# The second attention's output projection: six of eight head groups as one sum of two-level seven-product block multiplications

## The chip, the cores and the metric

The kernel runs on one core of a Trainium2 chip. The metric is the device time of one execution in microseconds (us); lower is better. All data are float32, and a matmul of float32 appears in the profile as two records. The engines are TensorE (PE; its weight loads are PEld), VectorE (DVE), ScalarE (ACT), GpSimd (POOL) and SyncE (SP), which issues nearly all DMAs.

## The reference, cut to what matters

Two decoder layers run over x of 4 x 256 tokens with 512 features, each an attention and a feed-forward part with a residual and a layernorm behind. The change is in the second layer's attention: 32 heads of value width 128, and an output projection `wo` of 4096 x 512.

```python
def _L1_attn_ref(hidden_states, wq, wkv, wo):
    ...
    probs = jax.nn.softmax(scores, axis=-1)
    attn = jnp.einsum('bhqk,bkhd->bqhd', probs, v).reshape(B, S, H * DV)
    return jnp.einsum('bse,ed->bsd', attn, wo)
...
x = _layernorm(x + _L1_attn_ref(x, L1_attn_wq, L1_attn_wkv, L1_attn_wo), axis=-1)
x = _layernorm(x + _L1_ffn_ref(x, ...), axis=-1)
```

The projection is one matrix product of 1024 tokens x 4096 by 4096 x 512. The kernel cuts the 4096 into eight groups `r` of four heads (512 rows each).

## The kernel before

The second layer's attention (from L1070) works in eight groups of four heads. While the softmax of group g runs, TensorE also makes the queries and keys of group g + 1; the units of that side work are spread over the sixteen (head, batch) steps `i` of the loop at L1546. Each step's result `att` goes by DMA to `attd[g]` in HBM (`output1`, L1442). In the last group the side work is the end of the queries and keys, and the projection of groups 0 and 1.

The projection of a group is `stages_o` (L1335): a block product after Winograd's form of Strassen's scheme. The left side is the group's attention output, transposed, 512 rows x 1024 tokens; the right side is `wo1[r]`, 512 x 512. Each is cut in two both ways, and seven products of blocks (256 rows x 512 tokens by 256 x 256) give what eight would. `ahead` (L1339) makes the sums and differences that the products need: four of 128x512 on the weights and four of 128x1024 on the attention output, on GpSimd (for group 0, the latter on VectorE). `product` (L1365) issues four matmuls of 256 columns for two token tiles; a group has two stages (`t0` of 0 and 2) of seven products, 56 matmuls. PSUM has three banks for it, and each product is evacuated at once: `plus` (L1377) adds it to the residual `x` on VectorE (L1379), and `last` adds the first product, kept in SBUF as `p1`, to three blocks of `x` on GpSimd (L1389).

Groups 2 to 7 follow behind the attention, one after the other (loop at L1631), with TensorE's program full of products; the next group's loads (`o_load`, `Weights.load`) and combinations run under them. Behind the last group come the layernorm of `x`, its transposes (`turned`), and the second feed-forward part: `routing` and `expert_linear` for each of the eight token tiles.

Where `pinned[0]` is set, instructions stay in program order on their engine; elsewhere the framework may reorder them by its own estimate. Tiles of a pool with the same tag share `bufs` buffers, and a new tile waits until the old one's readers are done; `slot` tiles come from a list of free numbers.

Of the kernel before, what the change touches and what calls it, by code (L numbers as in the profile page):

```python
# [9 lines left out]
F32 = mybir.dt.float32  # L10
# [3 lines left out]
ALU = mybir.AluOpType  # L14
# [3 lines left out]
P = 128  # L18
# [21 lines left out]
def tile_decoder2(ctx: ExitStack, tc: tile.TileContext, a: dict, out: bass.AP):  # L40
# [125 lines left out]
    def thirds(c):  # L166
        return [c[:, i] for i in range(3)]
# [904 lines left out]
    with tc.tile_pool(name="l1", bufs=2) as l1, tc.tile_pool(name="l1x", bufs=1) as l1x:  # L1072
# [250 lines left out]
        def o_load(r):  # L1323

            if r == 0:
                ov[0] = l1.tile([P, GH, N], F32, tag="v", name="att0")
                xo = l1x.tile([P, 5 * GH, Q], F32, tag="x2o", name="xo")
                ov[1] = xo[:, :4 * GH].rearrange("p (h t) c -> p h (t c)", t=4)
                odd = [xo[:, 4 * GH:], *(wts.tile([P, 4, Q], F32, tag=f"x2{i}", name=f"xo{i}", bufs=1) for i in (2, 0))]
                ov["c"] = ([  # L1330
                    l1x.tile([P, 2, HN], F32, tag=f"t{i}", name=f"to{i}") for i in (1, 3, 5)
                ], [t.rearrange("p (h t) c -> p h (t c)", t=2) for t in odd])
            nc.sync.dma_start(out=ov[r % 2], in_=attd[r])

        def stages_o(pr, r):  # L1335

# [118 lines left out]
        for g in range(NG):  # L1455
# [14 lines left out]
            if g > 1:  # L1470
# [2 lines left out]
                    nc.sync.dma_start(out=v[g], in_=vd[g])  # L1473

                sk[0]["load"] = values_of
        so = [stages_o(Weights(a["wo1"][r]), r) for r in range(NG)]
        flat = [st for grp in groups + [rest] + so for st in grp]
        for st, nxt in zip(flat, flat[1:]):
            if "ahead" in nxt and nxt is not so[0][0]:
                st["next"] = nxt["ahead"]  # L1480
        flat[0]["next"] = flat[3]["ahead"]
        del flat[2]["next"]
        for r in range(1, NG - 1):
            so[r][0]["att"] = lambda r=r: o_load(r + 1)
            so[r][0]["load"] = so[r + 1][0]["w"]

        def back(t0):

            for t in (t0, t0 + 2):
# [44 lines left out]
        for u, _ in units_of(groups[0]):  # L1534
            u()


        pending = turned_ = None
        for g in range(NG):
# [6 lines left out]
            for i in range(GH * B):  # L1546
# [11 lines left out]
                if last and i == 1:  # L1558
# [4 lines left out]
                    so[0][0]["ahead"]()  # L1563
                    o_load(1)
                    back(0)
        output1(*turned_)
        output1(*pending[:2], transposes1(pending[2]))


        iscale = 1.0 / math.sqrt(DK)  # L1570
        free[:] = [n for n in range(NSLOT) if n not in (*even, 5, 6, 7, 8)]

        def wslot(shape, src):
            t = slot(len(free), shape)
            nc.sync.dma_start(out=t, in_=src)
            return t

        wqk = [wslot([P, 2, 2 * E * DK], a["wqk"][:, 2 * k:2 * k + 2, :]) for k in range(2)]
        wA, wB = wslot([P, DC, E * R], a["wA"]), wslot([P, D], a["wB"])
        fb = wslot([P, D], a["rows"][:, 2, :])  # L1580
        wf = l1.tile([P, DC, D], F32, tag="v", name="wf")
        nc.sync.dma_start(out=wf, in_=a["wf"])

        def routing(t):

            xts = [xT[:, d, bass.ts(t, P)] for d in range(DC)]
            pqk = bank(f"b{t % 2}", (P, 2, E * DK))
            mm(pqk, [(xts[d], wqk[d // 2][:, d % 2, :]) for d in range(DC)])
            qs = l1.tile([P, E * DK], F32, tag="s5", name="qs", bufs=1)
            A.copy(qs, pqk[:, 0, :])  # L1590
            qk = l1.tile([P, E, DK], F32, tag="s6", name="qk", bufs=1)
            V.tensor_tensor(qk.rearrange("p e d -> p (e d)"), pqk[:, 1, :], qs, ALU.mult)
            se = small.tile([P, E], F32, name="se")
            V.tensor_reduce(se, qk, AX.X, ALU.add)
            nmx = small.tile([P, 1], F32, name="nmx1")
            V.tensor_reduce(nmx, se, AX.X, ALU.max, negate=True)
            nms = small.tile([P, 1], F32, name="nms")
            V.tensor_scalar(nms, nmx, iscale, None, ALU.mult)
            we = small.tile([P, E], F32, name="we")
            sm = small.tile([P, 1], F32, name="sm1")  # L1600
            A.activation(we, se, AF.Exp, bias=nms, scale=iscale, accum_out=sm)
            rc = small.tile([P, 1], F32, name="rc1")
            V.reciprocal(rc, sm)
            wn = small.tile([P, E], F32, name="wn")
            V.tensor_scalar(wn, we, rc, None, ALU.mult)
            return wn

        def expert_linear(t, wn, parts):
            xts = [xT[:, d, bass.ts(t, P)] for d in range(DC)]
            ph = bank("b2", (P, E, R))  # L1610
            mm(ph, [(xts[d], wA[:, d, :]) for d in range(DC)])
# [6 lines left out]
            G.tensor_tensor(x[:, t, :], x[:, t, :], fb, ALU.add)  # L1618

            st = small.tile([P, parts, 6], F32, name="sth")  # L1620
            for k in range(parts):
                cols = bass.ts(k, D // parts)
                po = bank("b2" if k else "o", (P, D // parts))
                mm(po, [(xts[d], wf[:, d, cols]) for d in range(DC)] + [(hwT, wB[:, cols])])
# [5 lines left out]
        halves = ((0, 1, 4, 5), (2, 3, 6, 7))  # L1630
        for r in range(2, NG):  # L1631
            for n, st in enumerate(so[r]):
                for u, _ in units_of([st]):
                    u()
                if r == NG - 1:
                    for t in halves[n]:
                        layernorm(t)
        for t in halves[0]:
            turned(t, A.copy)
        order = (*halves[0], *halves[1])  # L1640
        wn = routing(order[0])
        for n, t in enumerate(order):
            now = wn
            if n in (1, 2):
                for t1 in halves[1][2 * n - 2:2 * n]:
                    turned(t1, A.copy)
            if n + 1 < NT:
                wn = routing(order[n + 1])
            expert_linear(t, now, 2 if n == NT - 1 else 1)


def _layouts(i):
# [86 lines left out]
```

## Time and profile before

| | |
|---|---|
| time, median of 3 runs | 1588.53 us (1587.66 to 1590.2) |
| the profiled execution's own time | 1589.84 us |
| its span from the first to the last instruction | 1587.7 us |
| granted TensorE clock in it | 0.997 |
| busy: PE, DVE, ACT, POOL | 97%, 67%, 46%, 68% |
| projection of groups 2 to 7 | 1361.4 to 1506.45 us of the span |
| from there to the end | 81.25 us |

How to read the views that are shown below. The page's first part has the busy time of each engine. The chain that ended last follows the work back from the last instruction; in order of time, a line has the start, the length, the engine, the tile and the line of the kernel. A timeline line has start, length, engine, line, operation, out<-in and shape. A group line has the count, then busy time in us and the mean in ns of one, then the idle time before and what ended it. Matmuls are pipelined, so their recorded durations overlap and the distance between starts tells the rate.

### The profile page before, as it was taken

The numbers are of one execution on the slowest core, as the hardware profiler recorded it, in microseconds if no ns is written. First come the engines' busy times: TensorE is split into PE (matmuls) and PEld (weight loads), VectorE is DVE, ScalarE is ACT, GpSimd is POOL, SyncE is SP. The second block draws the span as 40 slices with busy tenths as digits, with TensorE's granted clock in tenths as the row PEclk, the third lists the DMA queues.
The fourth block names the chain that finished last, engine by engine and source line by source line (L and its number), as shares of the span: only waits on it lengthen the run. The fifth ranks groups of instructions, "written<-read, shape, count | busy, mean of one in ns | idle before, by whom it ended". The sixth has DMA issues, their size and how long they took to land.

```text
span 1587.7 us, 23217 instructions
## 1 busy us (share of the span) xinstructions
PE 1546.6 (97%) x7549; PEld 1221.9 (77%) x7549; DVE 1066.4 (67%) x2282; ACT 723.3 (46%) x2097; POOL 1084.3 (68%) x1299
## 2 busy tenths in 40 slices
PE   8999999999989999999999999999999999999998
PEld 5566666666567778888789999999999988888854
DVE  2677777776786577777777777777777775333454
ACT  1466666666664341111155555555555543100143
POOL 1988887883077148878687776868677777698520
PEclk9999999999999999999999999999999999999999
DMA  9365655552123036777332523425243154534000
GB/s 346 140 210 202 228 207 213 211 209 93 47 87 122 21 103 201 233 251 228 113 92 71 183 105 120 145 81 170 78 165 126 60 212 140 180 120 151 1 21 33
DMA packets 96620, 227.07 MB, mean 143 GB/s; under 512 B 10096, under 2 KB 53104, under 8 KB 90480
## 3 DMA queue, kind: packets, MB, share of 16 engines
q1 hardware_dynamic: 94832, 224.74, 41.4%
q8 instruction: 62, 1.02, 0.3%
q10 hardware_dynamic: 1664, 0.81, 0.2%
q14 instruction: 62, 0.51, 0.1%
HBM read 140.58 MB, written 84.93 MB: 142 GB/s over the span
## 4 chain that ended last, share of the span: by engine, by line
PE 61%; DVE 3%; POOL 2%; issue 1%; ACT 0%; DVEq 0%; ACTq 0%; POOLq 0%
PE ps_b L1183 21%; PE ps_b L1370 12%; PE ps_s L82 5%; PE ps_b L1280 5%; PE ps_o L1446 3%; PE ps_t L1437 3%; PE ps_t L1280 2%; PE ps_o L82 2%; PE ps_o L53 2%; PE ps_b L82 2%; PE ps_o L1447 2%; PE ps_o L1280 1%; PE ps_s L1280 1%; DVE x L1112 0%; DVE vb L1112 0%
## 5 line engine op out<-in xcount | busy, mean ns | idle before, releaser
L1419 ACT ACTIVATE pr<-ps_s,nmx 128x128 f32<-128x128 f32 (+1 forms) x256 | 105.3, 418 | 140.7 <-DVE nmx L1415 140.6
L1379 DVE TENSOR_TENSOR x<-ps_b,x 128x512 f32<-128x512 f32 x96 | 66.3, 691 | 109.3 <-PE ps_b L1370 101.9
L378 ACT ACTIVATE pr<-ps_s,ebias 128x256 f32<-128x256 f32 x256 | 118.0, 473 | 45.6 <-DVE ebias L373 43.7
L82 PE MATMUL ps_s<-kT,qh 128*128 128x256 f32 x512 | 128.6, 392 | 0.8 <-ACT pr L378 0.8
L82 PEld LDWEIGHTS ps_s<-kT,qh 128*128 128x128 f32 x512 | 91.7, 189 | 36.7 <-issue 20.2
L1112 DVE SCALAR_TENSOR_TENSOR x<-ps_b,p 128x512 f32<-128x512 f32 (+1 forms) x159 | 96.5, 608 | 21.7 <-PE ps_b L1183 9.5
L1431 ACT ACTIVATE pr<-pr,rc 128x128 f32<-128x128 f32 (+1 forms) x256 | 103.7, 455 | 14.2 <-DVE rc L1429 13.3
L160 POOL TENSOR_TENSOR ws<-ws 128x128 f32<-128x128 f32 (+1 forms) x128 | 70.8, 571 | 46.6 <-DMA ws<-in_wq 27.2
L393 DVE TENSOR_SCALAR pr<-pr,rc 128x256 f32<-128x256 f32 x192 | 98.9, 541 | 4.4
L367 DVE TENSOR_REDUCE nmx<-ps_s 128x2 f32<-128x512 f32 x128 | 85.0, 684 | 23.3 <-PE ps_s L82 22.8
L1439 DVE COPY pT<-ps_t 128x384 f32<-128x384 f32 x128 | 71.3, 557 | 35.5 <-PE ps_t L1437 33.6
L1389 POOL TENSOR_TENSOR x<-x,po 128x512 f32<-128x512 f32 x48 | 60.4, 1271 | 35.4 <-DVE x L1379 29.4
L1415 DVE TENSOR_REDUCE nmx<-ps_s 128x1 f32<-128x128 f32 (+1 forms) x256 | 79.5, 352 | 3.4
L1411 DVE TENSOR_TENSOR ps_s<-ps_s,mask 128x256 f32<-128x256 f32 x128 | 55.2, 431 | 36.5 <-PE ps_s L82 36.3
L1446 PE MATMUL ps_o<-pT,v 128*128 128x256 f32 x256 | 76.3, 380 | 0.1
L1112 DVE SCALAR_TENSOR_TENSOR x<-ps_b,x 128x512 f32<-128x512 f32 (+1 forms) x106 | 64.1, 607 | 17.0 <-PE ps_b L1183 10.6
L1109 ACT ACTIVATE p<-ps_b 128x512 f32<-128x512 f32 (+1 forms) x78 | 43.1, 553 | 69.7 <-PE ps_b L1183 36.3
L419 PEld LDWEIGHTS ps_o<-pT,cN 128*64 128x64 f32 x504 | 31.0, 136 | 55.4 <-issue 26.2
L419 PE MATMUL ps_o<-pT,cN 128*64 128x256 f32 x504 | 68.3, 391 | 4.3 <-DVE pT L406 4.3
L163 POOL TENSOR_TENSOR ws<-ws,ws 128x128 f32<-128x128 f32 (+1 forms) x128 | 70.4, 564 | 2.5
L162 POOL TENSOR_TENSOR ws<-ws 128x128 f32<-128x128 f32 (+1 forms) x128 | 71.0, 570 | 1.3
L161 POOL TENSOR_TENSOR ws<-ws 128x128 f32<-128x128 f32 (+1 forms) x128 | 69.8, 563 | 1.3
(699 smaller groups left out, 4495.2 us busy)
## 6 DMA issues: line engine op xcount, KB each, us to landing
attd<-att SPq DMA_DIRECT2D x128, 128.0 KB, 1.8
vw<-ws SPq DMA_DIRECT2D x56, 256.0 KB, 2.4
qd<-ws SPq DMA_DIRECT2D x56, 256.0 KB, 2.2
qb<-vw SPq DMA_DIRECT2D x28, 512.0 KB, 4.6
qb<-qd SPq DMA_DIRECT2D x24, 512.0 KB, 4.4
v<-vd SPq DMA_DIRECT2D x6, 2048.0 KB, 8.8
qc<-vw SPq DMA_DIRECT2D x28, 384.0 KB, 4.2
vw<-ws SPq DMA_DIRECT2D x24, 384.0 KB, 2.5
```

The source lines that it names most:

```text
L82: T.matmul(o, l, r, start=(i == 0), stop=(i == len(pairs) - 1))
L367: V.tensor_reduce(nmx[:, i, :], sc, AX.X, ALU.max, negate=True)
L378: A.activation(pr[:, i, qt, :], sc[:, qt, :], AF.Exp, bias=bias[:, i, qt:qt + 1], accum_out=sm[:, i, qt:qt + 1],)
L393: V.tensor_scalar(prs, prs, rc[:, i, qt:qt + 1], None, ALU.mult)
L419: T.matmul(po[i * RKV:(i + 1) * RKV, :], cN[:, 2 * b + kt, :], pTs[i][:, kt, :], start=(kt == 0), stop=(kt == 1),)
L1112: V.scalar_tensor_tensor(o[key], acc, scale, o[other], ALU.mult, ALU.add)
L1183: T.matmul(acc[:, e, :], pr.inner[i][k], inner[i][k], start=first and e == 0, stop=True, skip_group_check=True,)
L1280: T.matmul(acc[:, t, :].rearrange("p (h c) -> p h c", h=2), inner[i][k][:, t * P:(t + 1) * P], pr.inner[i][k], start=first and t == 0, sto ...
L1370: T.matmul(st[tag][:, tt, :], box["left"][i][:, k, (t0 + tt) * P:(t0 + tt + 1) * P], box["right"][i][:, k, :], start=first and tt == 0 and ...
L1419: A.activation(pr[:, pt, :], sc[:, pt, :], AF.Exp, bias=nmx[:, qt:qt + 1], accum_out=sm[:, qt:qt + 1],)
L1431: A.activation(pr[:, pt, :], pr[:, pt, :], AF.Copy, scale=rc[:, qt:qt + 1])
L1446: T.matmul(po, v[g][:, 2 * b, hv], pT[:, 0:2, :], start=True, stop=False)
```

## The change

Groups 0 and 1 stay as they were. Groups 2 to 7 are done together, and each by two levels of the seven-product scheme: the outer blocks are 256 rows x 512 tokens and 256 x 256, as before, and each of the seven outer products is done by seven inner ones (128 rows x 256 tokens by 128 x 128), 49 in all. The outer products are taken in four passes `p`, `OUTER = ((2, 0), (1, 4), (3, 6), (5,))`, and each pass goes through the six groups: 24 steps `(p, r)`. In a pass each inner product (of a pair of outer ones) has a PSUM bank to itself, in which it is summed over the six groups; `evacuate(p)` empties them behind the pass's last group. `sweep` issues a step's matmuls of 128 columns, 28 for a pair, 14 in the last pass.

The combinations are made in place where they can be: `base_left` and `outer_left` on GpSimd, on the loaded blocks of attention output; `base_right` and `outer_right` on VectorE, on the weights. `prepare_step` makes a step's inner combinations on VectorE, into the double-buffered tiles `c` and `cc`, one step ahead. `jobs` places the rest behind the steps. The sums of evacuated products are kept in `xs` and added to `x` by `post`. Part of the loads is moved into the last attention loop (`o_early`), the rest is queued behind step 0, and the last part's weights behind step 19. The last two attention outputs are done within step 0, and the layernorm and the transposes of tiles 0 to 3 within steps 19 to 23. `pinned[0]` is set throughout.

```diff
-            nc.sync.dma_start(out=ov[r % 2], in_=attd[r])
+            nc.sync.dma_start(out=ov[r], in_=attd[r])
...
-        so = [stages_o(Weights(a["wo1"][r]), r) for r in range(NG)]
+        so = [stages_o(Weights(a["wo1"][r]), r) for r in range(2)]
...
-        for r in range(1, NG - 1):
-            so[r][0]["att"] = lambda r=r: o_load(r + 1)
-            so[r][0]["load"] = so[r + 1][0]["w"]
...
+        RS = range(2, NG)
+        W = D // 4
+        LEFT = {0: (0, 0), 1: (0, 0), 2: (0, 1), 3: (1, 0), 4: (1, 0), 5: (1, 1), 6: (0, 1)}
+        RIGHT = {0: (0, 0), 2: (1, 0), 3: (0, 0), 4: (0, 1), 5: (1, 0), 6: (1, 1)}
+        JS = (0, 1, 4, 2, 6, 3, 5)
+        steps = [(p, r) for p in range(len(OUTER)) for r in RS]
+        L, RW, whole, u2s, combos, acc, spare = {}, {}, {}, {}, {}, {}, {}
+
+        def load_left(r, m, k, t):
+            b = t.rearrange("p (h c) -> p h c", h=2)
+            nc.sync.dma_start(out=b, in_=attd[r][:, 2 * k:2 * k + 2, m * HN:(m + 1) * HN])
+            L[r, m, k] = b
+
+        def load_right(r, n, t):
+            b = t.rearrange("p (h c) -> p h c", h=GH)
+            nc.sync.dma_start(out=b, in_=a["wo1"][r][:, :, 2 * n * W:2 * (n + 1) * W])
+            RW[r, 0, n], RW[r, 1, n], whole[r, n] = b[:, :2], b[:, 2:], b
+
+        def spot():
+            return l1.tile([P, N], F32, tag=f"s{free.pop(0)}", name="ob", bufs=1)
+
+        def base_left(r, m):
+
+            for k in range(2):
+                b = L[r, m, k]
+                G.tensor_tensor(b[:, 0, Q:], b[:, 0, Q:], b[:, 1, Q:], ALU.add)
+
+        def base_right(r, n):
+            b = whole[r, n].rearrange("p (k h) c -> p k h c", k=2)[:, :, 0, :]
+            V.tensor_tensor(b[:, :, W:], b[:, :, W:], b[:, :, :W], ALU.subtract)
+
+        def outer_left(r, which):
+            l11, l12, l21, l22 = (L[r, m, k] for m in range(2) for k in range(2))
+            o, l, rr, op = dict(
+                sum=(l21, l21, l22, ALU.add), s2=(l11, l21, l11, ALU.subtract),
+                s4=(l12, l12, l11, ALU.subtract), s3=(l21, l22, l11, ALU.subtract),
+            )[which]
+            G.tensor_tensor(o, l, rr, op)
+
+        def outer_right(r):
+            base_right(r, 1)
+            r11, r12, r21, r22 = (RW[r, k, n] for k in range(2) for n in range(2))
+            u2 = u2s[r] = wts.tile([P, 2, 2 * W], F32, tag="qc", name="u2", bufs=3)
+            V.tensor_tensor(r12, r12, r11, ALU.subtract)
+            V.tensor_tensor(u2, r22, r12, ALU.subtract)
+            V.tensor_tensor(r11, u2, r11, ALU.subtract)
+            V.tensor_tensor(r21, r21, u2, ALU.subtract)
+
+        def prepare_step(s):
+
+            p, r = steps[s]
+            if p == 0:
+                base_right(r, 0)
+            c = cmb.tile([P, 2, 3, Q], F32, tag="c", name="oc")
+            cc = cmb.tile([P, 2, 3, W], F32, tag="cc", name="occ")
+            for e, i in enumerate(OUTER[p]):
+                b = u2s[r] if i == 1 else RW[(r, *RIGHT[i])]
+                r11, r12, r21, r22 = b[:, 0, :W], b[:, 0, W:], b[:, 1, :W], b[:, 1, W:]
+                u2, u3, u4 = thirds(cc[:, e])
+                V.tensor_tensor(u2, r22, r12, ALU.subtract)
+                V.tensor_tensor(u3, u2, r11, ALU.subtract)
+                V.tensor_tensor(u4, r21, u2, ALU.subtract)
+                b = L[(r, *LEFT[i])]
+                l11, l12, l21, l22 = b[:, 0, :Q], b[:, 1, :Q], b[:, 0, Q:], b[:, 1, Q:]
+                s2, s3, s4 = thirds(c[:, e])
+                V.tensor_tensor(s2, l21, l11, ALU.subtract)
+                V.tensor_tensor(s4, l12, s2, ALU.subtract)
+                V.tensor_tensor(s3, l22, s2, ALU.subtract)
+                combos[s, e] = ((l11, s2, l12, s3, l21, l22, s4), (r11, u2, r21, u3, r12, u4, r22))
+
+        def sweep(s, js=JS):
+
+            p, r = steps[s]
+            pair = OUTER[p]
+            for j in js:
+                fresh = False
+                if r == RS[0]:
+                    k = JS.index(j)
+                    fresh = len(pair) == 2 or k % 2 == 0
+                    if fresh:
+                        spare[p] = bank("q", (P, 2, 2, W))
+                    acc[p, j] = spare[p] if len(pair) == 2 else spare[p][:, k % 2:k % 2 + 1]
+                for e in range(len(pair)):
+                    l, rr = combos[s, e]
+                    for t in range(2):
+                        T.matmul(
+                            acc[p, j][:, e, t, :], l[j][:, t * P:(t + 1) * P], rr[j],
+                            start=fresh and e == t == 0, stop=r == RS[-1], skip_group_check=True,
+                        )
+
+        def evacuate(p):
+
+            n = len(OUTER[p])
+            pick = (slice(0, 2), slice(0, 3, 2), slice(0, 3, 2), slice(0, 1))[p]
+            c00, c01, c10, c11 = (
+                spare["x"][:, pick, 2 * m:2 * m + 2, k * W:(k + 1) * W] for m in range(2) for k in range(2)
+            )
+            held = l1.tile([P, 2, 2, W], F32, tag="p1", name="held")[:, :n]
+            A.copy(held, acc[p, 0])
+            for o, j, other in (
+                (c10, 1, held), (c11, 4, c10), (c00, 2, held), (c01, 6, c11), (c11, 3, c11), (c10, 3, c10), (c10, 5, c10),
+            ):
+                V.tensor_tensor(o, acc[p, j], other, ALU.add)
+
+        def xb(m, k):
+            return x[:, 4 * m:4 * m + 4, 2 * k * W:2 * (k + 1) * W]
+
+        def post(eng, o, k):
+            eng.tensor_tensor(o, o, spare["x"][:, k], ALU.add)
+
+        def early(r, t):
+            load_left(r, 0, 0, t[0])
+            load_left(r, 0, 1, t[1])
+            load_right(r, 0, t[2])
...
+        o_early = {
+            3: lambda: (early(2, (xT[:, 0, :], xT[:, 1, :], qb())), early(3, (xT[:, 2, :], xT[:, 3, :], qb()))),
+            7: lambda: early(4, (spot(), spot(), qb())),
+            9: lambda: early(5, (spot(), spot(), tb(1))),
+            11: lambda: (early(6, (spot(), spot(), tb(3))), base_left(2, 0), base_left(3, 0)),
+            13: lambda: prepare_step(0),
+            15: lambda: prepare_step(1),
+        }
+
+        def o_rest():
+
+            vx, vy = (l1.tile([P, DC, N], F32, tag="v", name="ov") for _ in range(2))
+            for n, r in enumerate((2, 3)):
+                free.insert(0, even[n])
+                load_left(r, 1, 0, spot())
+                load_left(r, 1, 1, vy[:, n, :])
+            pinned[0] = True
+            ring.update(q=[0, 1, 2, 3, 4, 6, 5, 7], t=[5])
+            sweep(0, JS[:5])
+            output1(*turned_)
+            pT = transposes1(pending[2])
+            sweep(0, JS[5:6])
+            output1(*pending[:2], pT)
+            sweep(0, JS[6:])
...
+            for n, r in enumerate(RS):
+                for k in range(2 if r in last_left else 0):
+                    load_left(r, 1, k, last_left[r][k])
+                load_right(r, 1, last_right[n])
+                if r == 3:
+                    early(7, seven_)
+
+            jobs = {s: [] for s in range(len(steps))}
+            for n, r in enumerate(RS):
+                if r > 3:
+                    jobs[n - 2].append(lambda r=r: base_left(r, 0))
+            for n, r in enumerate(RS):
+                jobs[n + 1].append(lambda r=r: (base_left(r, 1), outer_left(r, "sum")))
+                jobs[(4, 5, 6, 7, 7, 8)[n]].append(lambda r=r: outer_left(r, "s2"))
+                jobs[(2, 3, 4, 7, 8, 9)[n]].append(lambda r=r: outer_right(r))
+                jobs[9 + n].append(lambda r=r: outer_left(r, "s4"))
+                jobs[10 + n].append(lambda r=r: outer_left(r, "s3"))
+            jobs[8].append(lambda: post(G, xb(0, 0), 0))
+            jobs[9].insert(0, lambda: post(G, xb(0, 0), 1))
+            jobs[13] += [
+                lambda: V.tensor_tensor(xs[:, 1], xs[:, 1], xs[:, 0], ALU.add),
+                lambda: V.tensor_tensor(xs[:, 2], xs[:, 2], xs[:, 1], ALU.add),
+            ]
+            jobs[15].append(lambda: post(G, xb(0, 1), 2))
+            jobs[16].append(lambda: post(G, xb(1, 1), 2))
+            jobs[18] += [
+                lambda: (post(V, xb(0, 1), 2), post(G, xb(1, 1), 0)),
+                lambda: G.tensor_tensor(xs[:, 1], xs[:, 1], xs[:, 0], ALU.add),
+                lambda: post(G, xb(1, 0), 1),
+            ]
+            jobs[19] += [last_weights, lambda: (layernorm(0, True), layernorm(2))]
+            jobs[20] += [lambda: (layernorm(1, True), layernorm(3))]
+            jobs[21] += [lambda: turned(0, A.copy), lambda: turned(2, A.copy)]
+            jobs[22] += [lambda: turned(1, A.copy)]
+            jobs[23] += [lambda: turned(3, A.copy)]
+            for s in range(len(steps)):
+                p, r = steps[s]
+                if s == 18:
+                    ring["t"] = [1, 2]
+                if s:
+                    sweep(s)
+                if s + 1 < len(steps) and s:
+                    prepare_step(s + 1)
+                if r == RS[-1]:
+                    evacuate(p)
+                for job in jobs[s]:
+                    job()
+            post(V, xb(1, 0), 0)
+            pinned[0] = False
...
+                if last and i in o_early:
+                    o_early[i]()
+        o_rest()
-        output1(*turned_)
-        output1(*pending[:2], transposes1(pending[2]))
...
-        for r in range(2, NG):
-            for n, st in enumerate(so[r]):
...
+        for t in range(4, NT):
+            layernorm(t)
+        ring.update(b0=[3], b1=[4], b2=[6], o=[5], t=[1, 2])
+        wn = routing(0)
...
```

More of the change, by code (lines that the diff above doesn't have):

```diff
@@ L1535, in tile_decoder2, with last_weights, load @@
             u()
+        last_w = {}
+        def last_weights():
+            def load(n, shape, src):
+                t = l1.tile(list(shape), F32, tag=f"s{n}", name="lw", bufs=1)
+                nc.sync.dma_start(out=t, in_=src)
+                return t
+            last_w["wqk"] = [load(k, [P, 2, 2 * E * DK], a["wqk"][:, 2 * k:2 * k + 2, :]) for k in range(2)]
+            last_w["wA"], last_w["wB"] = load(2, [P, DC, E * R], a["wA"]), load(3, [P, D], a["wB"])
+            last_w["fb"] = load(4, [P, D], a["rows"][:, 2, :])
+            last_w["wf"] = [load(9 + k, [P, 2, D], a["wf"][:, 2 * k:2 * k + 2, :]) for k in range(2)]
@@ new lines, in xb, with qb, tb @@
+        def xb(m, k):
[6 more added lines that the diff above has]
+            load_right(r, 0, t[2])
+        def qb():
+            return wts.tile([P, N], F32, tag="qb", name="ow", bufs=3)
+        def tb(k):
+            return l1x.tile([P, N], F32, tag=f"t{k}", name="ow")
@@ new lines, in tile_decoder2 @@
+        o_early = {
[20 more added lines that the diff above has]
+            sweep(0, JS[6:])
+            w = l1.tile([P, 2, N], F32, tag="w", name="ow", bufs=1)
+            xo = l1x.tile([P, 5 * GH, Q], F32, tag="x2o", name="ox")
+            xs = xo.rearrange("p (k t) c -> p k t c", t=GH)
+            spare["x"] = xs[:, :3]
+            last_right = [w[:, 0, :], w[:, 1, :]] + [xs[:, k].rearrange("p t c -> p (t c)") for k in (3, 4)]
+            last_right += [wts.tile([P, N], F32, tag=f"x2{i}", name="ow", bufs=1) for i in (2, 0)]
+            seven_ = (spot(), spot(), tb(5))
+            last_left = {4: (spot(), vy[:, 2, :]), 5: (spot(), vy[:, 3, :]), 6: (vx[:, 0, :], vx[:, 1, :]), 7: (vx[:, 2, :], vx[:, 3, :])}
+            for n, r in enumerate(RS):
[46 more added lines that the diff above has]
+            pinned[0] = False
@@ L1565, in tile_decoder2 @@
                     back(0)
-        output1(*turned_)
-        output1(*pending[:2], transposes1(pending[2]))
+                if last and i in o_early:
+                    o_early[i]()
+        o_rest()
         iscale = 1.0 / math.sqrt(DK)
[L1571 to L1582, printed above, removed]
         def routing(t):
@@ L1587, in routing @@
             pqk = bank(f"b{t % 2}", (P, 2, E * DK))
-            mm(pqk, [(xts[d], wqk[d // 2][:, d % 2, :]) for d in range(DC)])
+            mm(pqk, [(xts[d], last_w["wqk"][d // 2][:, d % 2, :]) for d in range(DC)])
             qs = l1.tile([P, E * DK], F32, tag="s5", name="qs", bufs=1)
@@ L1610, in expert_linear @@
             ph = bank("b2", (P, E, R))
-            mm(ph, [(xts[d], wA[:, d, :]) for d in range(DC)])
+            mm(ph, [(xts[d], last_w["wA"][:, d, :]) for d in range(DC)])
             hw = l1.tile([P, E, R], F32, tag="s7", name="hw", bufs=1)
@@ L1617, in expert_linear @@
             A.copy(hwT, tp)
-            G.tensor_tensor(x[:, t, :], x[:, t, :], fb, ALU.add)
+            G.tensor_tensor(x[:, t, :], x[:, t, :], last_w["fb"], ALU.add)
             st = small.tile([P, parts, 6], F32, name="sth")
@@ L1623, in expert_linear @@
                 po = bank("b2" if k else "o", (P, D // parts))
-                mm(po, [(xts[d], wf[:, d, cols]) for d in range(DC)] + [(hwT, wB[:, cols])])
+                mm(po, [(xts[d], last_w["wf"][d // 2][:, d % 2, cols]) for d in range(DC)] + [(hwT, last_w["wB"][:, cols])])
                 V.tensor_tensor(x[:, t, cols], po, x[:, t, cols], ALU.add)
@@ L1628, in expert_linear @@
             nc.sync.dma_start(out=out[t * P:(t + 1) * P, :], in_=x[:, t, :])
-        halves = ((0, 1, 4, 5), (2, 3, 6, 7))
-        for r in range(2, NG):
-            for n, st in enumerate(so[r]):
[L1633 to L1642, printed above, removed]
+        for t in range(4, NT):
+            layernorm(t)
+        ring.update(b0=[3], b1=[4], b2=[6], o=[5], t=[1, 2])
+        wn = routing(0)
+        for t in range(NT):
             now = wn
-            if n in (1, 2):
-                for t1 in halves[1][2 * n - 2:2 * n]:
+            if t in (1, 2):
+                for t1 in (2 * t + 2, 2 * t + 3):
                     turned(t1, A.copy)
-            if n + 1 < NT:
-                wn = routing(order[n + 1])
-            expert_linear(t, now, 2 if n == NT - 1 else 1)
+            if t + 1 < NT:
+                wn = routing(t + 1)
+            expert_linear(t, now, 2 if t == NT - 1 else 1)
 def _layouts(i):
```

## The prediction

> **What bounds the kernel now.** I read the page first, then the chain of waits in order of time, then the stage of the change by itself.
>
> The page, part 1 (busy time, share of the span, instructions of each engine):
>
> ```profile
> PE 1546.6 (97%) x7549; PEld 1221.9 (77%) x7549; DVE 1066.4 (67%) x2282; ACT 723.3 (46%) x2097; POOL 1084.3 (68%) x1299
> ```
>
> The chain that ended last (start, length, engine, tile, line, instructions), and the busy time of the stage from the first product of group 2 to the last of group 7 (PE, PEld, DVE, ACT, POOL, then clock, DMA share, GB/s):
>
> ```profile
> 1361.76 130.38 PE ps_b L1370 x604
> 1499.44 7.17 PE ps_b L1370 x32
> ```
>
> ```profile
> 1361.40:1506.45 145.05, 144.91 (x671) 126.91 (x670) 54.06 (x91) 9.29 (x18) 115.13 (x75) 1.00 0.30 112
> ```
>
> The projection of groups 2 to 7 is 145.05 us in which TensorE never waits and VectorE has 91 us to spare. So less TensorE work pays in full, until the other engines come due. Their prices decide here, and there are two questions: what a 128-column product costs, and what happens when VectorE and GpSimd both add tiles in SBUF.
>
> TensorE in order of time (start, length, count; ends are modelled, so starts count), and one group kept by shape (count, busy us, mean ns):
>
> ```profile
> 1400.45 3.62 PE L1370 MATMUL ps_b<-w,xo 128*128 128x256 f32 x16
> 1403.90 1.89 PE L1370 MATMUL ps_b<-cu,xo 128*128 128x256 f32 x8
> ```
>
> ```profile
> L82 PE MATMUL ps_b<-slot,xT 128*128 128x128 f32 x64 | 8.4, 275 | 0.0
> ```
>
> Sixteen records of 256 columns start over 3.45 us: 0.2157 us each. One product is two records (671 records for 6 x 56 products). The 128-column group is eight stretches of eight records, each with weights of its own: 8.4/8 = 1.05 us a stretch, so (1.05 - 0.275)/7 = 0.111 us a record.
>
> VectorE and then GpSimd in one early stretch, each adding two tiles that lie in SBUF:
>
> ```profile
> 573.93 0.41 DVE L53 TENSOR_TENSOR x<-xT 128x256 f32<-128x256 f32 x1
> 574.26 0.41 DVE L53 TENSOR_TENSOR x<-xT,x 128x256 f32<-128x256 f32 x1
> ...
> 594.58 0.95 DVE L608 TENSOR_TENSOR x<-t 128x256 f32<-128x256 f32 x1
> 595.46 0.94 DVE L607 TENSOR_TENSOR x<-t,x 128x256 f32<-128x256 f32 x1
> 596.33 1.75 DVE L1081 TENSOR_TENSOR t<-xT,t 128x1024 f32<-128x1024 f32 x1
> ```
>
> ```profile
> 594.40 0.85 POOL L609 TENSOR_TENSOR x<-xT,x 128x256 f32<-128x256 f32 x1
> 595.22 0.91 POOL L606 TENSOR_TENSOR x<-t 128x256 f32<-128x256 f32 x1
> 596.09 0.91 POOL L608 TENSOR_TENSOR x<-t 128x256 f32<-128x256 f32 x1
> 596.96 1.70 POOL L607 TENSOR_TENSOR x<-t,x 128x256 f32<-128x256 f32 x1
> ```
>
> Alone, VectorE's 128x256 takes 0.41 us and the next starts 0.33 later. Beside GpSimd it takes 0.95, and each engine's operation ends only after the other's has let go: they take turns. A pair costs 0.87 us, of which VectorE holds 0.28 and GpSimd 0.59. VectorE operations that read PSUM (0.69 us at L1379) show no such stretching. In the stage now VectorE's 54 us are nearly all of that kind, so this costs nothing today.
>
> GpSimd's prices at 128x1024 and 128x512, and VectorE's out of PSUM:
>
> ```profile
> L1357 POOL TENSOR_TENSOR xo<-xo 128x1024 f32<-128x1024 f32 x4 | 9.4, 2360 | 0.2
> L1347 POOL TENSOR_TENSOR cu<-w 128x512 f32<-128x512 f32 x4 | 5.1, 1270 | 0.3
> L1379 DVE TENSOR_TENSOR x<-ps_b,x 128x512 f32<-128x512 f32 x96 | 66.3, 691 | 109.3 <-PE ps_b L1370 101.9
> ```
>
> **TensorE.** Removed: 6 groups x 56 products x 2 x 0.2157 = 145.0 us. Added: per group 49 block products x 2 token tiles = 98 of 128 columns; 588 x 2 x 0.1115 = 131.1 us. Gain 13.9 us. A pair step (28 products) is 6.25 us, one of the last six 3.1. The row has only eight such records in a run, so the price may rise in a long one; never below 0.107 (half of 0.2157).
>
> By the Trainium skill, page "TensorE: Matmul & The Clock Gate", section "Back-to-back issue gap", a stream of weight load and matmul at 128 columns sustains about 81 ns against 56 isolated, 1.45 times as much. That speaks against this change: the products would take some 190 us (estimate by that page). The row shows 0.111 with a fresh load each time, so the row stands.
>
> **What VectorE gets.** Prices for two SBUF inputs: 128x256 0.33 start to start; 128x512 0.61; 128x1024 1.13 to 1.2 (L1356, alone). 128x128 has no row; on the line through these, 0.20. A result used at once adds 0.12. `prepare_step` for a pair is six of 128x128 and six of 128x256 with four such uses: 1.2 + 2.0 + 0.5 = 3.7 us; for the last, single steps 1.85. `outer_right` is one 128x256, four 128x512, two uses: 3.0 us. `evacuate` is 7 x 0.69 = 4.8 us out of PSUM, following the last sweep product by product. Before, 72 L1379 additions of 0.69 stood here.
>
> **What GpSimd gets.** `base_left` 0.77 us a piece (two per half), `outer_left` and posts 2.36 each. Removed are its 8 combinations and 6 posts a group (115 us); added in the stage 20 x 0.77 + 31 x 2.36 = 88.6 us.
>
> Neither engine alone passes TensorE. Together they do, as each VectorE addition waits in its queue for the GpSimd operation that is running, up to 2.36 us. Behind it stand the rest of the step's combinations, `outer_right` and the evacuation; TensorE's weight loads of the next sweep wait for them. There are two buffers of `c` and `cc`, so VectorE can be only one step ahead. I sum by quarters of six steps, GpSimd at what it holds (2.2 and 0.59 us), VectorE at its own pace less 0.1 for each operation that was queued behind GpSimd, and GpSimd's work free of charge while VectorE evacuates:
> - Steps 0 to 5: five prepares, four base combinations and three `outer_right`, 28.8 - 1.8 = 27 us; GpSimd 18 small and 7 large, 26 us, 5 of them during step 0 when VectorE has none of this. 48 us against 31.3 of TensorE (steps 1 to 5): 16.7 late.
> - Steps 6 to 11: six prepares, three `outer_right`, 31.2 - 1.2; evacuation 4.8; GpSimd 2 small, 12 large, 27.6 - 4.8. 57.6 against 37.5: 20 late.
> - Steps 12 to 17: 20.4 + 2.4 - 0.6; 4.8; GpSimd 9 large, 19.8 - 4.8. 42 against 37.5: 4.5 late.
> - Steps 18 to 23: 9.3 + 1.2, evacuation 4.8, two layernorms 3.4, GpSimd 1.8. 20.5 against 18.8: 1.7 late.
>
> Together 43 us late. Low end: only held time counts (2.5 us for a prepare or an `outer_right`): 10.8 + 12.5 + 0 + 0 = 23. High end: all at full duration, 22.9 + 23.5 + 6.5 + 2 = 55. I take 43, since the one alternating stretch in the trace runs at the held price while it alternates, and VectorE's many small operations run at their own pace when GpSimd's queue is empty.
>
> The Trainium skill ("SBUF — State Buffer", "Who interferes with whom") says that the loser blocks for the whole instruction; taken so, the sum would be the high end, 55. The trace's pair of 0.87 us, where both alone make 1.1, says that about a fifth overlaps.
>
> **Moved, or at nothing.** The loads are as many bytes; now 10.5 MB are queued after step 0. A 2 MB load took 8.8 us, so 44 us if they run like that, in step with the groups' use; at the stage's 112 GB/s they take 94 and the last groups wait, 0 to 12 us. I take 0. SP's queue in the last attention loop has the early loads between the stores of `att`; each waits for a tile that products due by then have read. Three `att` buffers cover that; 0 to 3 us if not, as a late store would hold L1449 and the next products. `prepare_step(0)` and `(1)` run there among the softmax; GpSimd loses group 2's 14.5 us of combinations in the same place: 0 to 3 us, taken as 0. The tail: transposes of tiles 0 to 3 move in front, the same TensorE time. VectorE still ends with four layernorms (1.7 us each), beside 7.8 us of routing products; -1 to 3, taken as 0. Last weights load from step 17 on, 2.8 MB, about 12 us under 18.8: nothing.
>
> **Sum.** -13.9 + 43 = +29 us. The profiled run took 1589.84 us (span 1587.7 and 2.1 around it), 1.3 above the median of 1588.53: 1619 on its scale, 1618 on the median's.
>
> **The rivals.**
> - *TensorE stays the bound, faster.* If turns are rarely taken, as GpSimd works while VectorE evacuates or waits, VectorE's 3.7 to 6.7 us a step fit under 6.25 and only some 2 us of sweep starts remain: 1588.5 - 13.9 + 2 = 1577. For it: each engine alone fits. Against: 23 us at held prices cannot be packed away. It decides if a large GpSimd operation held the tiles for less than about 0.8 us instead of 2.2. 0.12.
> - *Weight loads bound.* If a long run of 128 columns falls to a load's 0.19 us a record, the products take 223 us: +78, about 1667. Against: 64 records at 0.111. 0.02.
> - *The loads come late.* At 112 GB/s, 12 us on top of the lock: 1630. Against: early slices move over 200 GB/s. 0.10.
> - *About even*, gain and lateness cancelling (14 us late): 0.03.
>
> The forecast itself: 0.73. By 0.2% (3.2 us, about what a measurement of this kernel can tell from no change): faster 0.12, same 0.03, slower 0.85. The range: low end 1598 by held prices, taken down to 1592 for what GpSimd may do earlier; high end 1618 + 12 of the high prices + 10 of late loads or lost clock, 1640. Left out are the faster case, part of the even one, and about 5 in 100 above.
>
> **What would show it.** Products of 128 columns at 0.111 us a record in runs of 28; VectorE's 128x128 and 128x256 additions well over their 0.3 to 0.4 us mean, many near 2.5; TensorE idle of 2 to 5 us ahead of sweeps 2 to 12, ended by VectorE's combinations, and little in steps 18 to 23; the stage some 174 us long. TensorE over 95% busy through the stage, or VectorE's additions at their price alone, would prove it wrong; so would idle ended by DMA.

## The result and the profile after

| | before | after |
|---|---|---|
| time, median of 4 runs each | 1588.42 us (1587.66 to 1590.2) | 1652.38 us (1650.19 to 1655.0) |
| ratio | | 1.0402, 95% interval 1.0383 to 1.042 |
| span of the profiled execution | 1587.7 us | 1648.1 us |
| projection of groups 2 to 7 | 145.05 us | 206.7 us |
| from there to the end | 81.25 us | 76.4 us |

The change costs 64 us, 4.0%; the forecast was 1618 with a range up to 1640. The direction was right, the lateness was much too small. In the two profiled executions the span is 60.4 us longer: the stage begins 3.6 us later, takes 61.6 more, and what follows is 4.8 shorter, as the layernorms and transposes of tiles 0 to 3 and two of the tail's products now stand in front of the stage's end. The start of the stage varies: 1364.2 to 1377.6 us in the eight further profiles of kernels with the change. All nine are later than the 1361.4 of the one profile before, so whether part of the 3.6 us is an effect stays open.

The page, part 1, for the whole kernel after the change:

```profile
PE 1557.5 (95%) x8053; PEld 1248.4 (76%) x8053; DVE 1208.2 (73%) x2528; ACT 722.6 (44%) x2099; POOL 1048.0 (64%) x1270
```

VectorE's busy time has grown by 142 us and TensorE is still busy 95% of the time, so the page alone still points at TensorE. The stage shows otherwise. Steps 0 to 5, 6 to 11, 12 to 17 and 18 to 23 (columns as before: start:end, length, PE, PEld, DVE, ACT, POOL, then clock, DMA share and GB/s):

```profile
1364.99:1428.16 63.17, 46.92 (x349) 45.64 (x347) 60.16 (x75) 1.33 (x3) 44.41 (x32) 0.84 0.28 97
1428.16:1500.41 72.25, 49.62 (x338) 47.92 (x337) 70.56 (x111) 0.58 (x1) 35.01 (x14) 0.79 0.03 8
1500.41:1537.93 37.52, 37.52 (x338) 37.52 (x337) 32.39 (x77) 0.58 (x1) 7.22 (x3) 1.00 0.16 50
1537.93:1571.67 33.74, 27.21 (x188) 25.54 (x187) 25.68 (x56) 8.71 (x19) 11.13 (x6) 0.85 0.05 17
```

In the first half VectorE is the full engine: 60.2 of 63.2 us and 70.6 of 72.25. GpSimd has 32 operations in the first quarter and 14 in the second, and then only three. The third quarter runs at TensorE's pace, 37.52 us for six steps, which is 6.25 a step as forecast. The granted clock falls to 0.79.

What TensorE waits for in the stage (engine, tile and line, what for, us in total, times, longest):

```profile
PEld ps_q L53 <- DVE oc L53: 45.4, 13, 7.6
PE ps_q L53 <- DVE oc L53: 45.2, 14, 7.5
```

TensorE is idle for 45.4 us in the stage, and all but 0.2 of it ends with a left combination (`oc`) of VectorE. No wait for a DMA stands in this view, so the rival of late loads is out: it would have shown a wait behind the group's loads.

The chain that ended last, some of its long pieces in order of time (start, length, engine, tile, line):

```profile
1365.15 4.69 PE ps_q L53 x40
1383.98 4.96 DVE oc L53 x2
1444.34 4.93 DVE oc L53 x2
1493.35 43.86 PE ps_q L53 x372
```

Before, one piece of TensorE of 130 us stood here. Now VectorE's `oc` (the left combinations, `s2` to `s4`) and `occ` (the right ones) are in it, two additions of 128x256 for 4.9 us. The long piece of TensorE from 1493 us on is the third quarter.

One such piece from three sides, in the timeline of VectorE, GpSimd and TensorE (start, length, engine, line, operation, out<-in, shape; in brackets the idle time ahead):

```profile
1441.74 2.56 DVE L53 TENSOR_TENSOR oc<-xT 128x256 f32<-128x256 f32 x1
1444.34 4.93 DVE L53 TENSOR_TENSOR oc<-xT,oc 128x256 f32<-128x256 f32 x2
1449.19 2.42 DVE L53 TENSOR_TENSOR occ<-ow 128x128 f32<-128x128 f32 x1
1451.65 0.29 DVE L53 TENSOR_TENSOR occ<-occ,ow 128x128 f32<-128x128 f32 x1
```

```profile
1439.11 4.91 POOL L53 TENSOR_TENSOR x<-x,ox 128x1024 f32<-128x1024 f32 x2 [8.20 <-DVE ox L53]
1443.98 2.52 POOL L53 TENSOR_TENSOR xT<-xT 128x1024 f32<-128x1024 f32 x1
1446.46 2.52 POOL L53 TENSOR_TENSOR ob<-ov,xT 128x1024 f32<-128x1024 f32 x1
1448.95 2.52 POOL L53 TENSOR_TENSOR xT<-xT 128x1024 f32<-128x1024 f32 x1
```

```profile
1452.53 1.23 PE L53 MATMUL ps_q<-occ,oc 128*128 128x128 f32 x4 [7.46 <-DVE oc L53]
1453.55 1.06 PE L53 MATMUL ps_q<-u,xT 128*128 128x128 f32 x4
1454.40 1.06 PE L53 MATMUL ps_q<-ow,ob 128*128 128x128 f32 x4
```

For every addition of GpSimd here there is one of VectorE, which ends 0.1 to 0.3 us after GpSimd's. An addition of 128x128, 0.28 us alone, then takes 2.42. It is nearly one for one through the whole stage: GpSimd's 55 operations there stretch 52 of VectorE's. (Stretched means over 1.3 times the 0.285, 0.42, 0.69 and 1.22 us that 128x128, 128x256, 128x512 and 128x1024 take alone in these profiles.) The last fence shows something that was not forecast: behind the wait four records start over 0.85 us, 0.2125 each, nearly twice the 0.1117 of the other records.

### The profile page after: what moved, and what is told of

Read it like the earlier page. It is cut to its first block, busy times and chain, and to the rows that moved or that the text cites. A ratio compares the mean times of both kernels' runs of the same rounds, so it can differ in the third digit from the quotient of the medians.

```text
span 1648.1 us, 24448 instructions
## 1 busy us (share of the span) xinstructions
PE 1557.5 (95%) x8053; PEld 1248.4 (76%) x8053; DVE 1208.2 (73%) x2528; ACT 722.6 (44%) x2099; POOL 1048.0 (64%) x1270
## 4 chain that ended last, share of the span: by engine, by line
PE 54%; DVE 11%; issue 1%; POOL 1%; ACT 1%; DVEq 0%; ACTq 0%; POOLq 0%
PE ps_b L1183 20%; PE ps_s L82 5%; PE ps_b L1280 5%; PE ps_q L53 4%; PE ps_o L1446 3%; DVE occ L53 3%; DVE oc L53 3%; PE ps_b L1370 3%; PE ps_t L1437 2%; PE ps_b L82 2%; PE ps_t L1280 2%; PE ps_o L53 2%; PE ps_o L82 2%; PE ps_o L1447 2%; PE ps_o L1280 1%; PE ps_s L1280 1%
## 5 line engine op out<-in xcount | busy, mean ns | idle before, releaser
L160 POOL TENSOR_TENSOR ws<-ws 128x128 f32<-128x128 f32 (+1 forms) x128 | 70.7, 570 | 44.9 <-DMA ws<-in_wq 25.9
L393 DVE TENSOR_SCALAR pr<-pr,rc 128x256 f32<-128x256 f32 x192 | 94.8, 520 | 4.4
L53 PE MATMUL ps_q<-occ,oc 128*128 128x128 f32 x336 | 52.9, 298 | 45.0 <-DVE oc L53 45.0
L53 PEld LDWEIGHTS ps_q<-occ,oc 128*128 128x128 f32 x336 | 46.1, 208 | 48.2 <-DVE oc L53 44.9
L162 POOL TENSOR_TENSOR ws<-ws 128x128 f32<-128x128 f32 (+1 forms) x128 | 70.8, 568 | 1.3
```

Of the source, the lines that this page charges most:

```text
L53: return lambda *args, **kw: tc.keep_in_program_order(f(*args, **kw))
L393: V.tensor_scalar(prs, prs, rc[:, i, qt:qt + 1], None, ALU.mult)
```

## The experiments

The comparisons ran in two groups; the kernel before took 1589.65 us (median of 7) beside the first and 1589.7 us (median of 8) beside the second.

**1. Without GpSimd's left work** (`no_gpsimd`). `base_left` and `outer_left` issue nothing. GpSimd keeps eleven operations in the stage: seven additions of evacuated sums (128x1024, among them the `post`s) and four of 128x512.

```diff
-                G.tensor_tensor(b[:, 0, Q:], b[:, 0, Q:], b[:, 1, Q:], ALU.add)
+                pass
...
-            G.tensor_tensor(o, l, rr, op)
```

> base_left and outer_left issue nothing (the sums and differences on the attention output are left out; posts stay on GpSimd). Turns theory: VectorE's own work in the stage is about 94 us of two-input additions, 17 of evacuation and 8 of layernorm, under TensorE's 131, so the waits of 57 us and the half-clock records (18 us) nearly go: stage 140 to 150 us against 206.7, time about 1585 to 1595. Rival, VectorE's own chain (dependent small additions) is the bound: stage over 190, time over 1635. Rival, late loads: unchanged, about 1650.

Measured, one run: 1597.36 us, two above the expected interval. The stage by itself (columns as above) is four above its own:

```profile
1364.90:1518.90 154.00, 142.53 (x1206) 139.73 (x1205) 132.02 (x316) 11.11 (x24) 22.31 (x11) 0.97 0.18 59
```

Most of the loss is gone (52.7 of the stage's 61.6 us), so it is GpSimd's left work that makes it. But even with that work for nothing the kernel does not come below the one before. The eleven operations that GpSimd keeps still stretch nine of VectorE's additions, by 16.8 us in all. Of the 11.4 us for which TensorE waits, 8.1 come right behind such additions (steps 7, 19 and 22), and 3.3 behind a pair of layernorms. The last quarter takes 32.3 us, nearly what it takes after the change.

**2. Without VectorE's inner work** (`no_prepare`). `prepare_step` reuses the first two steps' combinations from step 2 on; all of GpSimd's operations and all loads stay.

```diff
+                if s > 1:
+                    (_, s2, _, s3, _, _, s4), (_, u2, _, u3, _, u4, _) = combos[s % 2, e]
+                    ...
+                    continue
```

> From step 2 on the inner combinations are not made (steps use those of step 0 or 1 in their place); GpSimd's work is all there. Turns theory: VectorE has some 45 us left, GpSimd's 89 us fit under TensorE: stage 138 to 148, time 1583 to 1595. Rival, GpSimd's work or the loads are late by themselves: stage over 165, time over 1610.

Measured, one run: 1584.43 us, within the expected interval; the stage is a little below it (columns as above):

```profile
1366.36:1503.47 137.11, 135.12 (x1202) 134.54 (x1201) 99.93 (x88) 11.22 (x24) 106.92 (x55) 1.00 0.19 66
```

All 55 operations of GpSimd are there and TensorE is busy for 135 of 137 us at full clock. So neither GpSimd, nor the loads, nor 128-column products are late by themselves. It takes both adders together. The stage is 7.9 us shorter than before's 145.05 and the kernel 5.2 us faster than the 1589.65 beside it: about that is what TensorE's saving is worth when nothing else is late.

**3. The left work on VectorE** (`left_on_vector`). In both lines of the first diff `G` becomes `V`; nothing is left out.

> base_left and outer_left on VectorE, nothing left out. Turns theory: VectorE then has 94 + 34 us of two-input additions, 17 evacuation, 8 layernorm, about 153 us, and hardly a collision: stage 155 to 168, time 1600 to 1614. Rival, VectorE's own chain is the bound: 34 us more than now, about 1686. Rival, late loads: about 1650.

Measured: 1625.34 us (1624.73 to 1638.57, 5 runs), ratio 1.0226 (1.0202 to 1.025). It is 27 us faster than the change, though VectorE now does all of it, and slower than expected. The mean of one kind of addition after the change, and then here, with one of the moved additions (group line: count, busy us, mean ns, idle):

```profile
L53 DVE TENSOR_TENSOR oc<-ob,oc 128x256 f32<-128x256 f32 x48 | 33.8, 745 | 0.8
```

```profile
L53 DVE TENSOR_TENSOR oc<-ob,oc 128x256 f32<-128x256 f32 x48 | 18.3, 421 | 0.8
L53 DVE TENSOR_TENSOR ob<-ob 128x1024 f32<-128x1024 f32 x6 | 7.3, 1218 | 0.0
```

A left combination of 128x1024 costs VectorE 1.22 us when it does it itself and over 2 us when GpSimd does it. The stage:

```profile
1377.60:1560.33 182.73, 153.44 (x1206) 147.84 (x1205) 166.65 (x360) 11.22 (x24) 23.27 (x11) 0.93 0.15 50
```

What is left is VectorE's load, 166.7 us busy in 182.7, but not its own alone: the expectation had "hardly a collision", and the eleven operations that GpSimd keeps stretch ten of VectorE's additions by 17.9 us. No run moves these to VectorE too. (The profiled execution is the slowest of the five, 1638.57 us; its stage begins at 1377.6, 12.6 us later than after the change, so the excess over the median lies ahead of the stage.)

**4. Clock kept up** (`filled`). Filler products into a spare bank are issued in the waits, as a test of whether the half pace behind the waits costs time.

```diff
+                    for _ in range(FILL.get((s, JS.index(j), e), 0)):
+                        ...
+                        T.matmul(fill[p][:, :2 * P], ident, mask.rearrange("p t c -> p (t c)"), start=True, stop=True)
```

> Matmuls of 256 columns into an unused bank are put where TensorE waited over 1.8 us (5 to 16 in each of ten places, about 0.5 us less than the wait), so that its clock stays granted; nothing else changes. If the 186 records at half clock (18.5 us) lie on the path: stage 188 to 196, time 1633 to 1641. If VectorE alone sets the pace and the slow products hide under its work: within 4 us of 1652.

Measured: 1654.12 us (1652.29 to 1655.41), ratio 1.0403 (1.0378 to 1.0428).

```profile
1370.45:1575.11 204.66, 183.42 (x1384) 172.91 (x1383) 188.07 (x316) 11.11 (x24) 98.20 (x55) 0.97 0.14 45
```

The clock in the stage rises from 0.85 to 0.97 and the records at the double distance fall from 186 to 35 (about 19 us of extra distance to 3.5). The kernel gains nothing. The stage is 2 us shorter only because two of the tail's products (four records), which stand inside it after the change, come behind it here: stage and tail together take 283.1 us after the change and 283.2 here. What the slow products took was time that TensorE would otherwise have waited for VectorE.

**5. Shorter turns** (`split_left`). Each `outer_left` is cut into four operations.

```diff
-            G.tensor_tensor(o, l, rr, op)
+            for h in range(2):
+                for c in range(2):
+                    part = slice(c * Q, (c + 1) * Q)
+                    G.tensor_tensor(o[:, h, part], l[:, h, part], rr[:, h, part], op)
```

> Each outer addition of a left operand on GpSimd (128x1024) is cut into four of 128x256; the values and the bytes are the same, only VectorE can come in between four times as often. If the two engines take turns instruction by instruction, so that a long GpSimd operation keeps a VectorE addition of two SBUF operands waiting for its whole length, VectorE is held for shorter times, GpSimd runs ahead less, and part of its work slides into steps 12 to 17: the stage goes from 206.7 to some 185 to 195 us and the kernel to 1630 to 1640. If only the total of GpSimd's busy time counts, the kernel stays at 1650 to 1655, or is a little longer for the 3 x 32 more instructions.

Measured: 1649.5 us (1647.8 to 1650.79), ratio 1.0372 (1.0355 to 1.039). The 1630 to 1640 were missed.

```profile
L53 DVE TENSOR_TENSOR oc<-ob 128x256 f32<-128x256 f32 x24 | 15.8, 657 | 0.0
L53 POOL TENSOR_TENSOR ob<-ob 128x256 f32<-128x256 f32 x36 | 30.5, 873 | 0.0
```

VectorE does get its turns: 122 of its additions are stretched instead of 52. But each is stretched by 0.58 us instead of 1.42, so all together by 71.1 us instead of 74.1. Only GpSimd pays for the shorter operations (125.7 us busy instead of 99.0). What VectorE loses goes with the work that GpSimd does, not with the number of pieces. The 3 us between this kernel and the change stay unclear, as the intervals of the two ratios overlap.

**6. GpSimd kept in step** (`in_step`). A small GpSimd copy ahead of each step's jobs reads the last combination of the next step's `prepare_step`.

```diff
+                if (s + 1, 0) in combos and jobs[s]:
+                    gate = small.tile([P, 1], F32, name="gate")
+                    G.tensor_copy(gate, combos[s + 1, len(OUTER[steps[s + 1][0]]) - 1][0][3][:, :1])
```

> Before the GpSimd work of each step one small GpSimd copy reads the last combination that VectorE makes in that step, so that GpSimd cannot run ahead of the step that its work was written in. If the excess of steps 0 to 11 over the forecast (21.6 us) comes mostly from GpSimd work that the forecast put into steps 12 to 17, those two quarters fall from 135.5 to about 122 us, the third quarter rises by 0 to 4, and the kernel takes 1638 to 1643. If running ahead costs nothing, it stays at 1650 to 1655; above that if the combinations then wait for GpSimd's operands.

Measured: 1643.71 us (1641.8 to 1648.1), ratio 1.0349 (1.0329 to 1.0369): 9 us less than the change, just above the expected 1638 to 1643. By quarters:

```profile
1364.80:1415.54 50.74, 44.72 (x349) 43.59 (x348) 43.84 (x75) 1.33 (x3) 29.16 (x27) 0.90 0.35 120
1415.54:1478.30 62.76, 48.10 (x339) 45.31 (x338) 61.24 (x100) 0.59 (x1) 34.95 (x23) 0.86 0.00 1
1478.30:1528.06 49.76, 42.35 (x339) 40.72 (x337) 48.58 (x84) 0.59 (x1) 28.81 (x17) 0.93 0.15 48
1528.06:1563.56 35.50, 27.15 (x188) 25.59 (x187) 28.49 (x60) 8.72 (x19) 13.32 (x11) 0.86 0.05 16
```

Steps 0 to 11 fall from 135.4 to 113.5 us, 21.9 less, about all of the excess over the forecast. Here 17 large additions of GpSimd stand in them, where the change has 25 and the forecast had 19, and the stretching there falls by 20.7, from 61.2 to 40.5 us. But steps 12 to 17 take 12.2 more, three times what was expected: eleven large additions of GpSimd now run there, and they stretch VectorE's by 19.4 us. Running ahead explains where the time was lost, and it is responsible for 9 of the 64 us. The rest of what steps 0 to 11 gain moves with the work into the later steps.

**7. The norms later** (`norm_late`). The layernorms of tiles 0 to 3 go behind the last combinations, the transposes behind them.

```diff
-            jobs[19] += [last_weights, lambda: (layernorm(0, True), layernorm(2))]
-            jobs[20] += [lambda: (layernorm(1, True), layernorm(3))]
...
+            jobs[19] += [last_weights]
+            jobs[22] += [lambda: (layernorm(0, True), layernorm(2)), lambda: (layernorm(1, True), layernorm(3))]
```

> The layer norms of tiles 0 to 3 are issued in step 22, behind the last combinations, instead of in steps 19 and 20. If the last quarter (33.7 us where 20.5 was forecast) is late because the norms' chains to ScalarE stand in VectorE's order ahead of the combinations of steps 21 and 22, it falls to about 25 us and the kernel to 1642 to 1649, less what the later norms put on the tail. If the quarter is late for GpSimd's operations alone, it stays over 30 us and the kernel at 1650 to 1658.

Measured: 1654.64 us (1651.91 to 1655.45), ratio 1.0405 (1.0387 to 1.0422). The last quarter and what follows it, first after the change, then with the norms later:

```profile
1537.93:1571.67 33.74, 27.21 (x188) 25.54 (x187) 25.68 (x56) 8.71 (x19) 11.13 (x6) 0.85 0.05 17
1571.67:1648.10 76.43, 70.73 (x243) 37.88 (x240) 41.46 (x131) 31.08 (x63) 6.30 (x5) 0.98 0.07 28
```

```profile
1541.24:1565.51 24.27, 20.81 (x172) 20.33 (x171) 19.49 (x42) 4.25 (x9) 7.31 (x3) 0.93 0.06 22
1565.51:1652.50 86.99, 76.97 (x258) 41.29 (x256) 45.61 (x144) 35.22 (x74) 10.30 (x8) 0.95 0.07 25
```

The quarter falls to 24.3 us, 9.5 less, as the first theory said, and the tail grows by 10.6. Of these, 6.2 are TensorE work that now stands in the tail (76.97 us busy against 70.73), since what reads the norms' results moves with them, and 4.3 are TensorE's idle time there (10.0 against 5.7). Of the quarter's 9.5 us, 3.3 are the wait behind the first pair of norms, 2.8 are records at the slow pace, and about 3 are transposes and two products of the tail that only changed their place. So the norms did make the quarter late, and yet nothing is won by moving them. The stage time alone would have called this a gain.

**8. Left work on VectorE and the norms later** (`vector_norm_late`): the edits of 3 and 7 together.

> All left additions on VectorE (1625.3 when done alone) and the layer norms of tiles 0 to 3 behind the last combinations. If both act on their own, the kernel takes 1612 to 1620. If the last quarter was late for GpSimd's operations alone, the norms bring nothing more and it stays at 1622 to 1628.

Measured: 1627.77 us (1626.79 to 1638.13), ratio 1.0261 (1.0225 to 1.0297). The norms bring nothing here either; the tail is 85.5 us long. The number falls where the rival put it, but its reason does not hold: the last steps did get shorter (18 to 23: 24.1 against 32.4 us in experiment 3), and the tail took it back, as in 7.

No run points to a version that beats the kernel before. With the whole left work on VectorE it takes 1625 us, and with that work for nothing 1597; only leaving out nearly all inner combinations (1584) gets below. A version in which GpSimd adds nothing at all in the stage was not run.

## Why the prediction was right or wrong

**The bound changes: right.** TensorE's idle time ends with VectorE's combinations, and it takes both adders: GpSimd's work costs nothing when VectorE's inner combinations are left out (experiment 2). Without GpSimd's left work 17 of the stage's 69.6 us above experiment 2 remain (experiment 1: 154.0 against 137.1), and 8.1 of the 11.4 us of waits even then stand behind collisions with what GpSimd keeps. No load is late, and the products keep their price.

**128-column products: right.** In the undisturbed third quarter 28 products take 6.25 us, 0.1117 us a record against 0.1115 forecast, over runs of hundreds of records. The term of -13.9 us stands, and the rival of weight loads is out.

**The price of one turn: right.** In steps 6 to 11, GpSimd's 14 large additions stretch 14 of VectorE's by 29.1 us in all: 2.08 each. The sum had 2.2 held less 0.1 for each queued operation, 2.1. The Trainium skill ("SBUF — State Buffer", "Who interferes with whom") says that a VectorE instruction with two SBUF inputs contends with a GpSimd instruction that reads SBUF, which these runs show. Of the page's full block ("Summary: rules for kernel authors": the one that issues second waits until the first is done) the trace shows nearly all: VectorE loses 2.08 us beside a GpSimd operation of 2.52 (the mean there), as its addition mostly starts 0.2 to 0.4 us after GpSimd's and ends 0.1 to 0.6 us after it.

**The sum by quarters: the step that failed.** It gave 54.3 (48, and 6.25 for step 0), 57.6, 42 and 20.5 us, 174.4 together. The trace has 63.2, 72.25, 37.5 and 33.7, which is 206.7. The missing 32.3 us:

- *How many of GpSimd's operations fall into the first half: +12.5, of which 4.5 came back.* The sum placed each operation in the step in which its line stands, 19 large ones in steps 0 to 11 and nine in steps 12 to 17. Nothing else holds GpSimd, and its queue runs as far ahead as its data allow: 25 large ones in steps 0 to 11, three in 12 to 17. Six more at 2.08 us are 12.5 in the half where VectorE had no room, and the third quarter, for which 4.5 us of lateness were forecast, had none. Experiment 6 holds GpSimd back, and steps 0 to 11 then take 113.5 us against the forecast's 111.9. Its first half has two large operations fewer than the sum placed there, so it does not separate this term from the next.
- *GpSimd's work "free of charge while VectorE evacuates": +7.9.* The sum took off 5 us in step 0 and 4.8 in the second quarter. The cover was not there. Behind the evacuation of pass 0 GpSimd's `post` operations wait for its results and hold up GpSimd's queue: it stands idle for 8.2 us up to 1439.11 (the bracket in the fence above) and starts again together with VectorE's combinations. In step 0 VectorE already makes combinations. Adding up every stretched addition of steps 0 to 11 gives 61.2 us, where the sum charged 40.8; the 20.4 between them are the 12.5 and, as the rest, these 7.9.
- *Steps 18 to 23: +13.2.* The sum had 18.8 us of products and 1.7 of lateness. The trace has 6.5 us of waits, about 4 of records at the slow pace, and 3.3 of transposes and of two products of the tail, which the sum did not have in the stage; about 1 is not resolved. The waits have two causes. One, 3.0 us in step 19, stands behind `prepare_step(19)`, which GpSimd's operations of the jobs of step 18 stretch (in all the quarter's stretching is 8.3 us, where GpSimd was charged with 1.8). The other, 3.3 us in step 21, stands behind the first pair of layernorms. Both pairs together were charged with 3.4 us of VectorE's time, but its queue keeps its order and waits inside them for ScalarE, and the first pair alone takes 4.8 us up to the next combination. From 1556.44 us on TensorE does not wait again. Experiment 7 shows that the norms' part is paid in the tail when they are moved.
- *Step 0: +2.15*, taken as nothing. TensorE does not wait there: eleven records for the last attention outputs (eight of products, three of transposes) stand in the step, which takes 8.40 us instead of 6.25. About 1.0 of steps 0 to 11 is left over.

Around the stage, the tail was taken as nothing and gained 4.8 us; the stage's start was taken as unchanged and came 3.6 us later.

**The range.** Its high end took GpSimd's operations at full duration and left their number and place as they were. The price was the part that was well known; the order of an in-order queue that nothing holds, and the cover, were the uncertain ones and had no bound of their own.

**Clock.** The range allowed 10 us for late loads or lost clock. The clock was lost (about 19 us of slower records), and experiment 4, which keeps it up, gains nothing, since VectorE set the pace.

## What to carry to other kernels

Where VectorE and GpSimd both add two float32 tiles from SBUF, as here, count every GpSimd operation as about 2 us of VectorE per 128x1024, wherever the two meet; unless something makes GpSimd wait, it meets VectorE as early as its data allow and not where its line stands. Work of this kind that VectorE does in 1.22 us is not relieved by giving it to GpSimd. And a stage that gets shorter is no gain until the tail has been read with it.

## What the runs showed of the hardware

Splitting a 128x1024 operation of GpSimd into four of 128x256 leaves VectorE's loss nearly unchanged (71.1 against 74.1 us), with 2.3 times as many collisions.

Behind many of the waits TensorE starts up to 27 records at 0.2125 us each instead of 0.112: 186 records in the stage. The granted clock of these stretches is 0.50, as in these two neighbours (columns as above, the clock third from the end):

```profile
1490.90:1497.60 6.70, 5.47 (x24) 5.18 (x25) 6.46 (x22) 0.00 (x0) 0.00 (x0) 0.50 0.06 23
1497.70:1500.40 2.70, 2.70 (x26) 2.70 (x25) 2.60 (x5) 0.00 (x0) 0.00 (x0) 1.00 0.00 0
```

In the first, four slow records stand behind a wait of 4.99 us and some twenty behind one of 0.64 that follows; in the second the pace is full again. So how many slow records stand behind a wait does not go by its length: where there are few, as also behind 4.5 us at 1396.22, TensorE had only four records to start before it waited again. The Trainium skill ("TensorE: Matmul & The Clock Gate", "Part 1: The HAM clock gate") says that the clock falls to half after an idle window of about 3.4 us, and that the windows run on by themselves, whenever the waits begin. The half in the row agrees with it; the length of the window is not measured here. Filling the waits with products that nobody needs brings the clock back to 0.97, and no time, as long as another engine is late.
